# Cross-attention block: scores in 32x64 tiles, value products in 64x32 tiles, maxima spread through DRAM

## The chip, the core and the metric

The kernel runs on one core of a Trainium2 chip. The metric is the time of one execution on the device in microseconds (us). The core has a matrix engine (TensorE, "PE" in the profile, its weight loads "PEld"), a vector engine (VectorE, "DVE"), an activation engine (ScalarE, "ACT"), a general engine (GpSimd, "POOL") and a queue that issues DMAs (SyncE, "SP"). Each engine takes its instructions in the order of the program and waits at the first whose inputs or buffers are not ready. TensorE writes to PSUM only, here eight banks of 128 x 512 floats.

## What is computed

One cross-attention layer in 32-bit floats. `x` is 16 x 1024 x 512, the context 16 x 64 x 512, and there are 16 heads of 32 features.

```python
xq  = ada_ln(x, cond)                 # normalise, then scale and shift by the condition
xkv = ada_ln(context, cond)
q = (xq @ Wq + bq)                    # (16, 1024, 16 heads, 32)
k, v = split(xkv @ Wkv + bkv)         # (16, 64, 16 heads, 32) each
scores = einsum('bqhd,bkhd->bhqk', q, k) / sqrt(32)
attn = softmax(scores)
out = einsum('bhqk,bkhd->bqhd', attn, v)
return x + (out @ Wp + bp)
```

## The kernel before

The queries are worked on in 32 blocks of 512 rows, two to a batch element. A block `i` passes through these steps:

- `load_x`, `q_stats`, `q_scale`, `hidden`: load the rows, take mean and variance (DVE), make the reciprocal deviation (a few tiny steps on ACT and POOL), normalise (ACT, L335).
- `turn`, `move`: transpose 32x32 pieces on DVE (L365) and put them together with 16 DMAs of 64 KB (L387), so that features lie on partitions. `scale_features` (ACT, L447) applies the condition.
- `query_product(i, 1..7)` (L539): q = xq Wq by seven half-size products instead of eight (Strassen's scheme), 4 matmuls of 128x128x256 each. POOL makes the sums that this needs (`feature_sums`, L498). `query_seed`, `query_out` (ACT) and `query_added` (DVE, L585) collect the parts.
- `scores(i, z)`: the 64 keys are taken in two halves z of 32. `score_products` (L658) runs 16 matmuls of a 32x32 tile for each half: row group r and column group c of the array hold one head each, so the 128 output partitions are 4 heads x 32 keys. `maximum` (DVE, L675) reduces over the 32 keys of each head while it transposes 32x32 pieces, and `copied` (ACT, L684) moves the scores to SBUF.
- `maxima`: the larger of the two halves (`both`, L695), spread again over 32 partitions by a transpose of a repeated operand into one 128x2048 tile (L704). `subtract` (POOL, L717) takes it from both halves, `weights` (ACT, L723) makes the exponentials.
- `total` (POOL, L757) adds the two halves, `row_total` (DVE, L762) sums over keys, `inverse_rows` takes the reciprocal and sends it through DRAM to the partitions of the output, `spread_rows` (L788) spreads it.
- `mix` (L826): 32 matmuls in 32x32 tiles, the two halves of the keys added in PSUM. `divided` (DVE, L806) scales them out of PSUM.
- `row_sums` (POOL, L930 to L935), `product(i, 1..7)` (L955), `added` (DVE, L979): the projection, again seven products, added to the residual and stored.

PSUM has two double banks "s", which scores and value products take in turn, and four single banks: 0 and 1 for the query products, 2 and 3 for the projection. The order of all work is written out by hand and the engines take it as it stands. The loop over `i` from 3 to 29 issues, for TensorE and with a = i-1, b = i-2, n = i+1, f = i+2 (numbers are the seven products):

```text
scores(i,0)  product(b,6)  query(n,1)  scores(i,1)  product(b,5)  product(b,4)
query(n,2)   product(b,3)  mix(a)      query(n,6)   product(a,1)  product(a,2)
query(n,7)   query(n,5)    query(n,4)  query(n,3)   product(a,7)
```

Blocks 0 to 2, the context keys and values and the last two blocks stand ahead of and behind the loop; block 29 is projected by four full products (`project`).

The two code paths that the change touches most read, before:

```python
for c in range(NC):
    nc.tensor.matmul(pss[r // 2][32 * c : 32 * c + 32, r % 2, :],
                     lhsT=kt[rows, c, z * HK : (z + 1) * HK], rhs=qt[rows, c, :], ...)
both(m, m_tiles.pop(i), ALU.max)
mb_tiles[i] = spread(i, m, f"mb_{i}", other=i == NB - 1)
```

Of the kernel before, what the change touches and what calls it, by code (L numbers as in the profile page):

```python
# [15 lines left out]
P = 128  # L16
# [4 lines left out]
def cross_attention_block(  # L21
# [566 lines left out]
    V_all = {g: kvpool.tile([P, PER, 2, P], F32, tag=f"V{g}", name=f"V_{g}") for g in GROUPS}  # L588
    for g, at in GROUPS.items():
        for bl in range(PER):  # L590
            k_tiles[at * PER + bl] = K_all[g][:, :, bl * LKV : (bl + 1) * LKV]
            v_tiles[at * PER + bl] = V_all[g][:, bl]
# [16 lines left out]
    def value_places(i, m, h, k):  # L609
        if i not in stages:  # L610
            stages[i] = wpool.tile([P, NT, H], F32, tag="WT", name=f"stage_{i}")
        dst = stages[i][:, 2 * h : 2 * h + 2, m * HO : (m + 1) * HO]
        return qa["v", k].rearrange("p (t f) -> p t f", t=2), dst

    def value_out(i, n):
        k, m, h = OUTS[n]
        src, dst = value_places(i, m, h, k)
        b = b_v_sb[:, m * HO : (m + 1) * HO]
        nc.vector.tensor_tensor(dst, src, b.unsqueeze(1).to_broadcast([P, 2, HO]), ALU.add)
# [6 lines left out]
    def value_move(i, m):  # L626
        for c in (2 * m, 2 * m + 1):
            for j in range(2):
                for z in range(2):
                    at = j * LKV + z * HK  # L630
                    nc.sync.dma_start(  # L631
                        V_all[i][32 * c : 32 * c + 32, j::2, z, :],
                        stages[i][at : at + HK, :, c * P : (c + 1) * P],
                    )
# [16 lines left out]
    def score_products(i, z):  # L651
# [3 lines left out]
        for r in range(HPC):  # L655
            rows = slice(32 * r, 32 * r + 32)
            for c in range(NC):
                nc.tensor.matmul(  # L658
                    pss[r // 2][32 * c : 32 * c + 32, r % 2, :],
                    lhsT=kt[rows, c, z * HK : (z + 1) * HK],  # L660
                    rhs=qt[rows, c, :],
                    start=True,
                    stop=True,
                )
        if z == 0:
            m_tiles[i] = small.tile([P, 2, HPC, NJ], F32, tag="m2", name=f"m2_{i}")
# [7 lines left out]
    def maximum(i, z, e):  # L674
        nc.vector.tensor_reduce(  # L675
            m_tiles[i][:, z, 2 * e : 2 * e + 2, :],
# [16 lines left out]
    def both(dst, src, op):  # L693

        nc.vector.tensor_reduce(dst, src.rearrange("p z r j -> p (r j) z"), AX.X, op)  # L695

    def spread(i, src, name, other=False):
        if other:

            t = qpool.tile([P, 4, NC, NT * 32], F32, tag="xt", name=name)  # L700
            t = t.rearrange("p g c n -> p (g c n)")
        else:
            t = rpool.tile([P, HPC * TB], F32, tag="spread", name=name)
        nc.vector.transpose(t, src.unsqueeze(2).to_broadcast([P, HPC * NJ, 32]))  # L704
        return t.rearrange("p (r q) -> p r q", r=HPC)

    mb_tiles = {}

    def maxima(i):

        m = small.tile([P, HPC * NJ], F32, tag="m", name=f"m_{i}")
        both(m, m_tiles.pop(i), ALU.max)
        mb_tiles[i] = spread(i, m, f"mb_{i}", other=i == NB - 1)

    def subtract(i, eng=nc.gpsimd, zs=(0, 1)):
        for z in zs:
            eng.tensor_tensor(s_tiles[i, z], s_tiles[i, z], mb_tiles[i], ALU.subtract)  # L717
# [3 lines left out]
    def weights(i, z):  # L721
        p = s_tiles[i, z]
        nc.scalar.activation(p, p, AF.Exp, scale=SCALE)  # L723

    def sums(i, z):
        if z == 0:
            l_tiles[i] = small.tile([P, 2, HPC, NJ], F32, tag="l2", name=f"l2_{i}", bufs=1)
        nc.vector.tensor_reduce(
            l_tiles[i][:, z],
            s_tiles[i, z].rearrange("p r (j a) -> p r j a", a=32),  # L730
# [5 lines left out]
    vb_tiles = {}  # L736

    def inverse(i):

        v = small.tile([P, HPC * NJ], F32, tag="v", name=f"v_{i}")  # L740
        both(v, l_tiles.pop(i), ALU.add)
        nc.vector.reciprocal(v, v)
        vb_tiles[i] = spread(i, v, f"vb_{i}", other=i == NB - 1)

    def divide(i, eng=nc.gpsimd):
        vb = vb_tiles.pop(i)
        for z in range(2):
            eng.tensor_tensor(s_tiles[i, z], s_tiles[i, z], vb, ALU.mult)


    sum_tiles, lt_tiles, vt_rows = {}, {}, {}

    def total(i):

        pool, tag = (xpool, "x") if i == NB - 2 else (big, f"big{(i + 1) % 2 * 2}")
        t = pool.tile([P, HPC, TB], F32, tag=tag, name=f"sum_{i}")
        nc.gpsimd.tensor_tensor(t, s_tiles[i, 0], s_tiles[i, 1], ALU.add)  # L757
        sum_tiles[i] = t

    def row_total(i):  # L760
        lt_tiles[i] = small.tile([P, HPC, NJ], F32, tag="lt", name=f"lt_{i}")
        nc.vector.tensor_reduce(  # L762
            lt_tiles[i],
            sum_tiles.pop(i).rearrange("p r (j a) -> p r j a", a=32),
            AX.X,
            ALU.add,
            apply_transpose=True,
        )

    def halves_total(i):  # L770
        lt_tiles[i] = small.tile([P, HPC, NJ], F32, tag="lt", name=f"lt_{i}")
        both(lt_tiles[i].rearrange("p r j -> p (r j)"), l_tiles.pop(i), ALU.add)

    def inverse_rows(i):

        lt = lt_tiles.pop(i)
        nc.vector.reciprocal(lt, lt)
        v = small.tile([P, NC, NJ], F32, tag="vr", name=f"vr_{i}")
        d = dram.tile([NC, 32, HPC, NJ], F32, tag="lt", name=f"ltd_{i}")
        nc.sync.dma_start(d.rearrange("c a r j -> (c a) r j"), lt)  # L780
        for r in range(HPC):
            nc.sync.dma_start(v[32 * r : 32 * r + 32], d[:, :, r, :].rearrange("c a j -> a c j"))
        vt_rows[i] = v

    def spread_rows(i):
        v = vt_rows.pop(i).rearrange("p c j -> p (c j)")
# [6 lines left out]
    def divided(i):  # L793
        vb = vb_tiles.pop(i)
        pool, tag = (big, "big2") if i == NB - 2 else (opool, "ot")
        ot = pool.tile([P, NC, TB], F32, tag=tag, name=f"ot_{i}")
        ot_tiles[i] = ot
        po = po_tiles.pop(i)
        for e in range(len(po)):
            if len(po) == NC:  # L800
                nc.vector.tensor_tensor(ot[:, e, :], po[e], vb[:, e, :], ALU.mult)
                if e < 2:
                    biased(i + 1, 2 + e)
            else:
                cs = slice(2 * e, 2 * e + 2)
                nc.vector.tensor_tensor(ot[:, cs, :], po[e], vb[:, cs, :], ALU.mult)  # L806
# [3 lines left out]
    def mix(i, apart=True, ks=(None,) * NC):  # L810
# [10 lines left out]
        for z in range(2):  # L821
            p = s_tiles.pop((i, z))
            for c in range(NC):
                rows = slice(32 * c, 32 * c + 32)
                for r in range(HPC):
                    nc.tensor.matmul(  # L826
                        po[c][32 * r : 32 * r + 32, :],
                        lhsT=vt[rows, z, 32 * r : 32 * r + 32],
# [784 lines left out]
```

## Time and profile before

| | |
|---|---|
| median of 2 runs | 1030.69 us (1029.12 to 1032.26) |
| the profiled execution | 1030.86 us, of which the span from first to last instruction is 1029.1 |
| PE busy | 1009.3 us, 8077 matmul passes |
| DVE, ACT, POOL busy | 860.9, 638.6, 805.9 us |
| DMA | 149.82 MB, mean 146 GB/s |
| granted clock of TensorE | 0.998 |

Busy time is the union of an engine's instructions. A 32-bit matmul appears as two records, one for each pass. Behind a group stand its count, its busy time, the mean of one instruction in ns and the idle time of the engine just before it, with what ended that.

### The profile page before, as it was taken

The numbers are of one execution on the slowest core, as the hardware profiler recorded it, in microseconds if no ns is written. First come the engines' busy times: TensorE is split into PE (matmuls) and PEld (weight loads), VectorE is DVE, ScalarE is ACT, GpSimd is POOL, SyncE is SP. The second block draws the span as 40 slices with busy tenths as digits, with TensorE's granted clock in tenths as the row PEclk, the third lists the DMA queues.
The fourth block names the chain that finished last, engine by engine and source line by source line (L and its number), as shares of the span: only waits on it lengthen the run. The fifth ranks groups of instructions, "written<-read, shape, count | busy, mean of one in ns | idle before, by whom it ended". The sixth has DMA issues, their size and how long they took to land.

```text
span 1029.1 us, 21212 instructions
## 1 busy us (share of the span) xinstructions
PE 1009.3 (98%) x8077; PEld 763.4 (74%) x8077; DVE 860.9 (84%) x1174; ACT 638.6 (62%) x1025; POOL 805.9 (78%) x518
## 2 busy tenths in 40 slices
PE   8999899999999999999999999999999999999998
PEld 7877556777777777777777778777777777777746
DVE  6686669889888888889898888898888888876795
ACT  3786565666666666667666666666666676665530
POOL 4566687798888888898888888988888888987861
PEclk9999999999999999999999999999999999999999
DMA  9563544444544444445444444445434444335122
GB/s 318 179 188 119 149 122 136 157 157 156 165 155 121 143 128 154 152 152 166 140 134 146 150 133 153 156 159 165 148 110 151 134 154 154 113 125 166 46 85 85
DMA packets 112197, 149.82 MB, mean 146 GB/s; under 512 B 34104, under 2 KB 45392, under 8 KB 112096
## 3 DMA queue, kind: packets, MB, share of 16 engines
q1 hardware_dynamic: 111712, 147.94, 45.3%
q8 instruction: 64, 1.05, 0.4%
q0 software_dynamic: 384, 0.54, 0.3%
q14 instruction: 37, 0.30, 0.1%
HBM read 79.21 MB, written 34.60 MB: 111 GB/s over the span
## 4 chain that ended last, share of the span: by engine, by line
PE 81%; SPq 6%; DMA 5%; DVE 4%; ACT 1%; issue 1%; POOL 1%; DVEq 0%; ACTq 0%; POOLq 0%
PE pp L955 34%; PE pq L539 33%; PE po L826 6%; PE ps L658 6%; SPq L387 4%; DMA ltd<-lt 1%; SPq L631 1%; PE pk_A L539 1%; PE pv_A L539 1%; DMA xt<-ht 1%; DMA r<-in_x_dram 1%; DVE ht L365 1%; DVE lt L762 1%; DMA wss_kv<-in_L_xcond_Wss_kv_dram 1%; DMA x<-in_x_dram 1%
## 5 line engine op out<-in xcount | busy, mean ns | idle before, releaser
L717 POOL TENSOR_TENSOR s<-s,mb 128x2048 f32<-128x2048 f32 x64 | 290.2, 4558 | 129.3 <-DVE mb L704 127.7
L684 ACT COPY s<-ps 128x1024 f32<-128x1024 f32 x128 | 129.4, 1012 | 108.1 <-DVE m L675 64.8
L675 DVE TRANSPOSE_TENSOR_REDUCE m<-ps 128x32 f32<-128x1024 f32 x128 | 150.7, 1213 | 33.6 <-PE ps L658 33.4
L955 PE MATMUL pp<-w_p_sb,ot 128*128 128x256 f32 x720 | 165.6, 379 | 0.5 <-DVE r L979 0.4
L979 DVE TENSOR_TENSOR r<-pp,r 128x512 f32<-128x512 f32 x203 | 131.8, 670 | 30.9 <-PE pp L955 24.3
L578 ACT ACTIVATE qt<-pq,bias_t 128x256 f32<-128x256 f32 x256 | 105.6, 463 | 77.2 <-PE pq L539 77.0
L955 PEld LDWEIGHTS pp<-w_p_sb,ot 128*128 128x128 f32 x720 | 136.6, 190 | 20.5 <-issue 1.6
L723 ACT ACTIVATE s<-s 128x2048 f32<-128x2048 f32 x64 | 122.3, 1911 | 43.8 <-POOL s L717 43.8
L757 POOL TENSOR_TENSOR sum<-s,s 128x2048 f32<-128x2048 f32 x31 | 140.7, 4540 | 7.0 <-ACT s L723 7.0
L955 PEld LDWEIGHTS pp<-WT,s 128*128 128x128 f32 x480 | 86.5, 189 | 57.0 <-issue 37.7
L539 PE MATMUL pq<-xt_sums,w_q_sums 128*128 128x256 f32 x512 | 123.3, 385 | 0.0
L539 PE MATMUL pq<-xt,w_q_sums 128*128 128x256 f32 x512 | 121.1, 379 | 1.6 <-DVE qt L585 1.6
L539 PE MATMUL pq<-xt,w_q_sb 128*128 128x256 f32 x512 | 121.6, 380 | 0.3 <-ACT pq L551 0.2
L539 PEld LDWEIGHTS pq<-xt_sums,w_q_sums 128*128 128x128 f32 x512 | 94.9, 190 | 36.5 <-issue 24.8
L955 PE MATMUL pp<-WT,s 128*128 128x256 f32 x480 | 119.3, 391 | 0.2 <-POOL s L934 0.2
L955 PE MATMUL pp<-WT,ot 128*128 128x256 f32 x480 | 113.6, 379 | 0.6 <-POOL ot L931 0.6
L539 PEld LDWEIGHTS pq<-xt,w_q_sb 128*128 128x128 f32 x512 | 96.8, 190 | 16.4 <-issue 1.7
L539 PEld LDWEIGHTS pq<-xt,w_q_sums 128*128 128x128 f32 x512 | 97.2, 190 | 15.2 <-DVE qt L585 2.0
L955 PEld LDWEIGHTS pp<-WT,ot 128*128 128x128 f32 x480 | 91.0, 190 | 14.1 <-POOL ot L931 1.0
L335 ACT ACTIVATE x<-x,rstdq 128x512 f32<-128x512 f32 x128 | 97.0, 807 | 4.4 <-POOL rstdq L312 4.4
L447 ACT ACTIVATE xt<-xt,ss_q 128x512 f32<-128x512 f32 x124 | 93.9, 808 | 5.1 <-DMA xt<-ht 4.5
L498 POOL TENSOR_TENSOR xt_sums<-xt 128x512 f32<-128x512 f32 x64 | 81.4, 1272 | 14.2 <-ACT xt L447 7.3
(176 smaller groups left out, 1509.8 us busy)
## 6 DMA issues: line engine op xcount, KB each, us to landing
x<-in_x_dram SPq DMA_DIRECT2D x32, 1024.0 KB, 5.5
r<-in_x_dram SPq DMA_DIRECT2D x32, 1024.0 KB, 5.1
xt<-ht SPq DMA_DIRECT2D x488, 64.0 KB, 2.0
out_dram<-r SPq DMA_DIRECT2D x58, 512.0 KB, 3.7
out_dram<-r SPq DMA_DIRECT2D x11, 256.0 KB, 2.2
wss_kv<-in_L_xcond_Wss_kv_dram SPq DMA_DIRECT2D x4, 512.0 KB, 7.3
wss_q<-in_L_xcond_Wss_q_dram SPq DMA_DIRECT2D x4, 512.0 KB, 11.0
vr<-ltd SPq DMA_DIRECT2D x128, 8.0 KB, 1.6
```

What stands on the lines that cost most here:

```text
L335: nc.scalar.activation(dst, src, AF.Identity, bias=rstd[:, 1, j : j + 1], scale=rstd[:, 0, j : j + 1])
L447: nc.scalar.activation(xt[:, :, c, :], xt[:, :, c, :], AF.Identity, scale=ss["q"][:, c, b : b + 1], bias=ss["q"][:, NC + c, b : b + 1],)
L498: eng.tensor_tensor(dst, a, b, ALU.subtract)
L539: nc.tensor.matmul(out_, lhsT=lhsT, rhs=rhs, start=new and m == 0 and c == 0, stop=c == HC - 1, skip_group_check=True,)
L578: nc.scalar.activation(dst, src, AF.Identity, bias=bq_t[:, o : o + 1])
L675: nc.vector.tensor_reduce(m_tiles[i][:, z, 2 * e : 2 * e + 2, :], s_banks[i, z][e].rearrange("p r (j a) -> p r j a", a=32), AX.X, ALU.max, ...
L684: nc.scalar.copy(s_tiles[i, z][:, 2 * e : 2 * e + 2, :], s_banks[i, z][e])
L717: eng.tensor_tensor(s_tiles[i, z], s_tiles[i, z], mb_tiles[i], ALU.subtract)
L723: nc.scalar.activation(p, p, AF.Exp, scale=SCALE)
L757: nc.gpsimd.tensor_tensor(t, s_tiles[i, 0], s_tiles[i, 1], ALU.add)
L955: nc.tensor.matmul(acc[k][:, t * HO : (t + 1) * HO], lhsT=rows[:, c, t * P : (t + 1) * P], rhs=cols[:, c, :], start=n == 2 and t == 0 and ...
L979: nc.vector.tensor_add(r, a, r)
```

## The change

Scores and value products use larger tiles, and the heads are divided in another way.

- A score half is now two groups of heads over all 64 keys, not all heads over 32 keys. Half `z` takes chunks z and 2+z of the features: 8 matmuls of 32 rows x 64 columns. The value product has 64 rows (keys) x 32 columns: 16 matmuls in place of 32, with nothing added up in PSUM. The value tiles are laid out to match, in 4 larger DMAs a group instead of 16.
- A head's 64 keys lie on two 32-partition groups. `maxima(i, w)`, now called for each half, copies the neighbouring group's maxima over (two copies of 32x64), takes the larger, transposes 128x64 (L709), stores it in DRAM by two DMAs (L712), and `spread_maxima` reads it back by two DMAs (L719) that repeat a row for 64 partitions, into the single tile "spread". The transpose of 128x2048 is gone; only for the last block (`wide`) the old way is kept, with four copies.
- `total` is gone. `sums` (DVE, L736) runs on each half; `rows_out`, `rows_in` carry the sums through DRAM, and `inverse` (L762, L766) adds the two groups and takes the reciprocal afterwards.
- The output of `mix` is no longer scaled on its way out of PSUM by DVE. `mixed` copies it (ACT, L818), two instructions a block, and `scaled` multiplies (POOL, L822).
- `product(b, 2)` starts from a copy of bank 2 (`product_seed`, ACT, L896).
- The projection of a block runs a whole loop step after its value product: `mix(a)` stands in the middle of the step, all seven products of `b` around it. Block 29 takes the seven products like the others. The order of blocks 0 to 2, the context and the end is written anew.

```diff
     def score_products(i, z):
-            for c in range(NC):
+            for u in range(2):
                 nc.tensor.matmul(
-                    pss[r // 2][32 * c : 32 * c + 32, r % 2, :],
-                    lhsT=kt[rows, c, z * HK : (z + 1) * HK],
-                    rhs=qt[rows, c, :],
+                    pss[r // 2][LKV * u : LKV * (u + 1), r % 2, :],
+                    lhsT=kt[rows, 2 * u + z, :],
+                    rhs=qt[rows, 2 * u + z, :],
...
+    pair = const.tile([P, HPC * NJ], F32, name="pair")
+    def maxima(i, w, wide=False):
+        m2 = m_tiles.pop((i, w)).rearrange("p r j -> p (r j)")
+        m = small.tile([P, HPC * NJ], F32, tag="m", name=f"m_{i}_{w}")
+        for k in range(4):
+            if wide or k % 2 == 0:
+                o = k + 1 - 2 * (k % 2)
+                nc.vector.tensor_copy(pair[32 * k : 32 * k + 32], m2[32 * o : 32 * o + 32])
+        nc.vector.tensor_tensor(m, m2, pair, ALU.max)
+        if wide:
+            t = rpool.tile([P, HPC * TB], F32, tag="spread", name=f"mb_{i}_{w}")
+            nc.vector.transpose(t, m.unsqueeze(2).to_broadcast([P, HPC * NJ, 32]))
+            mb_tiles[i, w] = t.rearrange("p (r q) -> p r q", r=HPC)
+            return
+        mt = small.tile([P, 2, 32], F32, tag="mt", name=f"mt_{i}_{w}", bufs=2)
+        nc.vector.transpose(mt.rearrange("p h a -> p (h a)"), m)
+        d = dram.tile([2, 2, 32, 32], F32, tag="m", name=f"md_{i}_{w}")
+        for u in range(2):
+            nc.sync.dma_start(d[u].rearrange("h x a -> x h a"), mt[LKV * u : LKV * u + HK])
+    def spread_maxima(i, w):
+        d = m_rows.pop((i, w)).rearrange("u h x a -> u (h x a)")
+        t = rpool.tile([P, HPC * TB], F32, tag="spread", name=f"mb_{i}_{w}")
+        for u in range(2):
+            nc.sync.dma_start(
+                t[LKV * u : LKV * (u + 1)], d[u : u + 1].to_broadcast([LKV, HPC * TB])
+            )
...
     def mix(...):
-        for z in range(2):
-            for c in range(NC):
-                rows = slice(32 * c, 32 * c + 32)
+        for w in range(2):
+            for u in range(2):
+                rows = slice(LKV * u, LKV * (u + 1))
                 for r in range(HPC):
                     nc.tensor.matmul(
-                        po[c][32 * r : 32 * r + 32, :],
-                        lhsT=vt[rows, z, 32 * r : 32 * r + 32],
+                        po[2 * u + w][32 * r : 32 * r + 32, :],
+                        lhsT=vt[rows, w, 32 * r : 32 * r + 32],
                         rhs=p[rows, r, :],
-                        start=(z == 0),
-                        stop=(z == 1),
+                        start=True,
+                        stop=True,
                     )
+    def mixed(i, e):
+        nc.scalar.copy(ot_tiles[i][:, 2 * e : 2 * e + 2, :], po_tiles[i][e])
+    def scaled(i, e):
+        ot, vb = (t[i][:, 2 * e : 2 * e + 2, :] for t in (ot_tiles, vb_tiles))
+        nc.gpsimd.tensor_tensor(ot, ot, vb, ALU.mult)
```

The new loop step, engine by engine:

```text
PE    query(n,1) scores(i,0) query(n,2) product(b,1) scores(i,1) query(n,6) query(n,7)
      product(b,2) query(n,5) product(b,6) product(b,7) mix(a) query(n,3)
      product(b,5) product(b,4) product(b,3) query(n,4)
DVE   maximum(i,0,1) statistic maximum(i,0,0) maxima(i,0) sums(a,1) maximum(i,1,0)
      maximum(i,1,1) maxima(i,1) statistic added(b,2) 2 statistics 3 turns added(b,6)
      query_added(n,5) added(b,7) turn inverse(a) added(b,5) spread_rows(a) sums(i,0)
      added(b,4) query_added(n,4) added(b,3)
ACT   query_seed(n) biased(b,2) copied(i,0,0) copied(i,0,1) weights(a,1) product_seed(b)
      query_out(n,2) copied(i,1,1) hidden query_out(n,6) copied(i,1,0) hidden scale
      query_out(n,7) 2 scales biased(b,3) hidden scale weights(i,0) q_scale query_out(n,3)
      mixed(a,0) mixed(a,1) hidden
POOL  row_sums(b,0) row_sums(b,1) subtract(i,0) 3 feature_sums(f) q_scale subtract(i,1)
      scaled(a,0) feature_sums(f) scaled(a,1)
SP    md(i,0) x2, mb(i,0) x2, ltd(a), md(i,1) x2, residual(a), vr(a) x4, mb(i,1) x2,
      x(i+5), move(i+3) x16, out(b) x2
```

Each `row_sums` is two instructions; the second of `row_sums(b,1)` overwrites what product(b,2) reads and waits for it. `scores(i+1,0)` needs `query_added(i+1,4)`.

## The prediction

> **What bounds the kernel now.** I read the page first: the busy shares, then the chain that ended last.
>
> ```profile
> PE 1009.3 (98%) x8077; PEld 763.4 (74%) x8077; DVE 860.9 (84%) x1174; ACT 638.6 (62%) x1025; POOL 805.9 (78%) x518
> ...
> PE 81%; SPq 6%; DMA 5%; DVE 4%; ACT 1%; issue 1%; POOL 1%; DVEq 0%; ACTq 0%; POOLq 0%
> ```
>
> TensorE hardly idles and most of the chain is its own. A window of one block of the loop says the same. Behind the stretch stand its length and the busy time of PE, PEld, DVE, ACT and POOL:
>
> ```profile
> 544.04:573.22 29.18, 29.18 (x241) 22.30 (x240) 25.87 (x35) 19.16 (x31) 24.38 (x16) 1.00 0.48 153
> ```
>
> The score matmuls of blocks 4 and 30 start at 193.74 and 952.75, so a block takes 759.0 / 26 = 29.19 us. What fills it, from TensorE's timeline (start, length, count):
>
> ```profile
> 571.42 1.89 PE L955 MATMUL pp<-WT,ot 128*128 128x256 f32 x8
> 573.24 1.14 PE L658 MATMUL ps<-qt,K_B 32*32 32x512 f32 x32
> 574.31 0.48 PE L955 MATMUL pp<-WT,s 128*128 128x256 f32 x1
> ...
> 584.32 1.89 PE L955 MATMUL pp<-WT,ot 128*128 128x256 f32 x8
> 586.14 2.35 PE L826 MATMUL po<-s,V_B 32*32 32x512 f32 x64
> ```
>
> One wide product (8 records: 4 matmuls of two passes) follows another every 1.727 us, so 14 of them take 24.18. A score half takes 1.07 (573.24 to 574.31), and the wide products before and after it are 0.09 and 0.11 longer: 1.27. The product with the values takes 2.28 and the same 0.2: 2.47. 24.18 + 2 x 1.27 + 2.47 = 29.19: TensorE is the bound. GpSimd waits 127.7 / 31 = 4.1 us per block:
>
> ```profile
> POOL s L717 <- DVE mb L704: 127.7, 31, 8.6
> ```
>
> **The change, part by part.** S is the start of a block's scores.
>
> *Tiles.* In a score half the 16 first passes start 6.7 ns apart, the second passes 0.454 after them, the next product 0.516 after the last: 0.454 + 0.100 + 0.516 = 1.07. Eight tiles, still 512 columns in two passes, shorten the middle term to 0.05: a half costs 1.22. The value product has two such rounds; the old second round began 0.52 after the last pass of the first. Eight tiles save between 0.13 (two shorter skews, other gaps kept) and 0.43 (that gap closed); I take 0.27, so 2.20. No 32x64 tile is in the trace: were the two tiles of a row group to run one after the other, a half would cost two more passes, 0.85. By TensorE alone: 24.18 + 2.44 + 2.20 = 28.82 us per block, 0.37 less.
>
> *Work moved.* Per block DVE loses the spreading transpose (2.24), the two halves' maximum (0.30) and the two scalings out of PSUM (2.28), and gains one sum (2.24) and two `maxima` of four small instructions, 0.16 to 0.20 each by L237 and L316, 0.8 each: 25.9 becomes about 24.9. ACT gains two 0.91 copies and a 0.5 seed: 21.5. POOL trades one 4.54 addition for two scalings of half the size: even. DMA gains 2 MB, 72 GB/s over 29 us beside 153, and SP 8 issues of about 0.43, which its queue (16 moves at 0.63) has room for. All lies under TensorE.
>
> *The wait it adds.* `subtract` now waits for maxima that go to DRAM and back. From the end of `maxima`: a store like `ltd<-lt` (1.5 us), then two 512 KB reads, which I put at 5.0 together (1 MB loads land in 5.1): 6.7 with the issues. The upper bank's maximum ends at S + 4.6 (1.34 after the scores, 1.13, a 0.9 statistic, 1.21). Without hindrance `maxima` ends at S + 5.4 and the first subtraction could start at S + 12.1; POOL is only free at S + 12.6, after the last row sum, which waits for product 2. Behind it in POOL's queue stand three feature sums, the second subtraction, both scalings and the next row sums, with 4 us of slack. So far it is hidden.
>
> *What takes the cover away.* While the context keys are made, DVE and POOL both run two-input operations on SBUF, POOL's first and DVE's second:
>
> ```profile
> 22.90 1.72 POOL L472 TENSOR_TENSOR w_k_sums<-w_k_sums,w_k_sb 128x512 f32<-128x512 f32 x1
> 24.57 1.72 POOL L472 TENSOR_TENSOR wv_sums<-wv_sums,w_v_sb 128x512 f32<-128x512 f32 x1
> ...
> 27.93 1.27 POOL L472 TENSOR_TENSOR w_k_sums<-w_k_sb,w_k_sums 128x512 f32<-128x512 f32 x1
> ```
>
> ```profile
> 24.01 1.16 DVE L498 TENSOR_TENSOR xk_sums_A<-xk_A 128x512 f32<-128x512 f32 x1
> 25.20 1.64 DVE L498 TENSOR_TENSOR xk_sums_A<-xk_A,xk_sums_A 128x512 f32<-128x512 f32 x1
> ```
>
> DVE's operations end at 25.17 and 26.84, both times 0.55 after POOL's instruction in progress ended (24.62, 26.29): they stood still until then. POOL's take 1.72 in place of 1.27: they waited for DVE. The two take turns. In today's loop no DVE instruction reads two SBUF operands. In the new `maxima` the maximum (L702) does and will be blocked. For its two 32x64 copies (L701) there is no row: at the low end 0.17 (L237, also one SBUF input), at the high end one POOL instruction each, 1.3 beside the row sums. The nearest large row is this one-input SBUF operation:
>
> ```profile
> 11.51 0.54 DVE L344 TENSOR_SCALAR x_A<-x_A,rstdq 128x512 f32<-128x512 f32 x1
> ```
>
> It takes 0.54 for 512 elements where a statistic (L294) takes 0.68: (0.54 - 0.17) / 504 is 0.73 ns an element, faster than the 1.0 of one an element in the other rows, so it reads SBUF more broadly than they do. I take the high end.
>
> The Trainium skill ("SBUF — State Buffer", Who interferes with whom) says that copies of this kind can also enter a mode that takes the ports shared with GpSimd for the whole instruction; the trace shows this for two inputs (the 0.55 above), not for a copy. By that rule the sum is 1100; were only two-input operations blocked, 1030.
>
> *The walk.* POOL ends the last scaling near S + 3.9, then runs three row sums of 1.3. The first copy is issued at S + 4.6 and goes at 5.2, the second at 6.65, the maximum at 8.1; `maxima` ends at 8.45, not 5.4. Two loops follow.
> - DVE to ACT to PE: sums to 10.7, next maximum to 11.85, then on ACT a copy 0.91, normalise 0.71, scale 0.71, query output 0.71, two scales 1.41, `biased` 0.52: 16.9. TensorE is at product 7 at S + 14.55: a stall of 2.35, a block of 31.2.
> - POOL: the subtraction starts at 8.45 + 6.7 = 15.15; then 4.5, 4.0 (feature sums), 1.1, 4.5, 2.3, 1.3, 2.3 = 20.0 to the last scaling; then 4.55 to the end of the next `maxima` and 6.7: 31.25.
> I take 31.2: 2.0 more than now.
>
> *The ends.* Scores of block 3 start at 162.6 now, those of block 31 at 974.3, and 54.8 remain. The new start lacks three products of block 1 and has one query product more (-3.5), the tiles save 0.8, blocked maxima cost some 2.7: 161. The end: the value product comes later and no query work is left to cover, so TensorE stands about 8 us before product 7 of block 29 (the last maxima wait for the first subtraction), 3.5 before product 1 of block 30 and 2 to 3 elsewhere. By the order of the list and the durations above that is 63, with blocking 64. 161 + 28 x 31.2 + 64 = 1098.6. The profiled run is 1030.86 for a span of 1029.1 (median of the runs 1030.69), so 1.8 lies around it: **1100**.
>
> **The rivals.**
> - *Only the maximum is blocked.* `maxima` ends near 5.8, POOL keeps slack, blocks take 28.82: 158.3 + 807 + 63 + 1.8 = 1030. For it: small copies are short (L237); the GpSimd slack of 4.1. Against: L344. 0.25; 1018 to 1045.
> - *Faster.* Small tiles lose the 0.2 around a half and the value product comes to 1.75: 28.0 a block, shorter end: 158 + 784 + 59 = 1001. It decides if `maxima` ends before S + 6 as well. Against it the skew terms. 0.05.
> - *A collision with the subtraction.* The second `maxima` starts at S + 12.95, 2.2 before the 4.5 us subtraction. Were the spread to land 2.2 earlier, a copy would wait 4.5 and the maximum another 1.35: product 7 at 21.9, blocks of 36: 161 + 1008 + 66 = 1235. 0.08.
> - *The tiles do not overlap.* 0.85 on each of four rounds: 32.2 a block, 158 + 902 + 63 = 1123. 0.05; every small tile in the trace overlaps.
>
> **How the numbers follow.** The forecast has 0.57. Its own range is 1062 (both copies pass in one turn: 30.0 a block, 1065) to 1150 (reads 1.8 slower). The range leaves out the faster case, the collision and a little of the first rival, 0.16: 1022 to 1160. A measurement here tells about 2% from no change (1010 to 1051): faster 0.06, same 0.24, slower 0.70.
>
> **What would show it.** L701 and L702 with means of 0.6 to 1.5 us while POOL is busy, 0.2 while it idles; TensorE idle before L931 (product 7), released by ACT's `pp` copy; a period near 31; POOL waiting for DMA `mb`. Copies of 0.2 throughout and a period under 29 would prove me wrong, as would value products above 2.5.

## The result and the profile after

The kernel after takes 1207.24 us (median of 2 runs, 1206.82 to 1207.66) against 1030.69: 1.171 times as long, 95% interval 1.163 to 1.179. It is slower, as forecast, but by 177 us and not by 69; 1100 was recorded, with 1160 as the upper end.

The page of the kernel after, first the busy shares and then the chain that ended last:

```profile
PE 1063.8 (88%) x6053; PEld 781.2 (65%) x6053; DVE 953.2 (79%) x1345; ACT 703.8 (58%) x1117; POOL 798.4 (66%) x545
...
PE 36%; DVE 22%; DMA 21%; POOL 13%; issue 3%; ACT 3%; SPq 3%; POOLq 0%; DVEq 0%; ACTq 0%
```

TensorE's share of the chain fell from 81% to 36%; DVE, DMA and POOL hold 56%. No single engine is busy all the time: this is the look of a ring, in which each waits for another once per block. The window over 26 blocks of the loop (start of the scores of block 4 to those of block 30; columns: length, then busy time of PE, PEld, DVE, ACT and POOL, granted clock, DMA share, GB/s):

```profile
231.94:1099.59 867.65, 785.88 (x4577) 582.12 (x4577) 735.04 (x995) 549.52 (x843) 635.01 (x409) 0.96 0.71 191
```

A block takes 867.65 / 26 = 33.37 us, where it took 29.19. PE is busy for 785.88 / 26 = 30.23 of it and idle for 3.14. TensorE's own work was to be 28.82 by the forecast; the last experiment below runs blocks in 28.73. So the 4.18 us are: -0.46 for the tiles, +1.50 for slower products, +3.14 for idling.

Three stretches tell where the 176.7 us between the two spans went. Here and in the table of runs, "start" is the time at which the scores of block 3 begin, "block" is the time from there to the scores of block 31 divided by 28, and "end" is the rest of the span:

| | start | block | end |
|---|---|---|---|
| before | 162.6 | 28.99 | 54.8 |
| forecast for the change | 161 | 31.2 | 64 |
| after | 196.6 | 33.26 | 77.9 |

The forecast missed 35.6 in the start, 57.7 in the loop and 13.9 at the end.

The small instructions of `maxima` stood still, as forecast. First the groups of the two lines (behind the bar: busy time, mean of one in ns; then idle time before them), then a block on DVE and on POOL (start, length):

```profile
L701 DVE COPY pair<-m 32x64 f32<-32x64 f32 x132 | 95.1, 720 | 3.1
L702 DVE TENSOR_TENSOR m<-m,pair 128x64 f32<-128x64 f32 x64 | 71.9, 1124 | 2.2
```

```profile
703.04 2.83 DVE L701 COPY pair<-m 32x64 f32<-32x64 f32 x2
705.91 2.30 DVE L702 TENSOR_TENSOR m<-m,pair 128x64 f32<-128x64 f32 x1
708.24 0.25 DVE L709 STREAM_TRANSPOSE mt<-m 128x64 f32<-128x64 f32 x1
```

```profile
702.25 2.35 POOL L822 TENSOR_TENSOR ot<-ot,vb 128x1024 f32<-128x1024 f32 x1
704.56 1.27 POOL L498 TENSOR_TENSOR xt_sums<-xt,xt_sums 128x512 f32<-128x512 f32 x1
705.78 2.35 POOL L822 TENSOR_TENSOR ot<-ot,vb 128x1024 f32<-128x1024 f32 x1
708.09 1.26 POOL L908 TENSOR_TENSOR s<-ot 128x512 f32<-128x512 f32 x1
```

The first copy ends with the first scaling (704.6), the second with the feature sum (705.8), the maximum with the second scaling (708.1). One POOL instruction each, in turns. But the instructions met are the scalings of 2.35, not the row sums of 1.3: the last scaling ends 9.2 us after S in the mean of blocks 4 to 29, where I had S + 3.9. Over the same blocks the first `maxima`, from the first copy to the end of the maximum, take 4.63 us in the mean, the second 0.91, and 0.65 where POOL is idle.

What TensorE waits for is not what I forecast. From the list of waits (total, times, longest):

```profile
PE pp L931 <- POOL ot L822: 76.5, 27, 5.4
PE pp L931 <- ACT pp L890: 20.9, 12, 8.8
```

The wait for ACT's `pp` copy ahead of product 7 is there, but small; the large one is product 1, which waits for the first scaling on POOL. That stands behind the second subtraction, and both subtractions wait for `mb` from DRAM (`POOL s L725 <- DMA mb<-md` 117.0 us, before 127.7 for DVE's spread). From the end of the transpose at 708.49 to the subtraction at 718.31 the trip takes 9.8 us, where I had 6.7:

```profile
718.31 4.57 POOL L725 TENSOR_TENSOR s<-s,mb 128x2048 f32<-128x2048 f32 x1 [2.24 <-DMA mb<-md]
```

### The profile page after: what moved, and what is told of

The parts are those of the page before. It is cut to its first block, busy times and chain, and to the rows that moved or that the text cites. A ratio compares the mean times of both kernels' runs of the same rounds, so it can differ in the third digit from the quotient of the medians.

```text
span 1205.8 us, 17690 instructions
## 1 busy us (share of the span) xinstructions
PE 1063.8 (88%) x6053; PEld 781.2 (65%) x6053; DVE 953.2 (79%) x1345; ACT 703.8 (58%) x1117; POOL 798.4 (66%) x545
## 3 DMA queue, kind: packets, MB, share of 16 engines
HBM read 145.27 MB, written 36.67 MB: 151 GB/s over the span
## 4 chain that ended last, share of the span: by engine, by line
PE 36%; DVE 22%; DMA 21%; POOL 13%; issue 3%; ACT 3%; SPq 3%; POOLq 0%; DVEq 0%; ACTq 0%
PE pp L931 15%; PE pq L539 12%; POOL s L725 10%; DMA mb<-md 7%; DVE m L671 6%; DVE pair L701 4%; DMA md<-mt 4%; DMA ltd<-l 4%; DMA x<-in_x_dram 4%; PE ps L655 3%; DVE m L702 3%; DVE l L736 3%; POOL ot L822 3%; PE po L803 2%; PE pv_A L539 1%
## 5 line engine op out<-in xcount | busy, mean ns | idle before, releaser
L725 POOL TENSOR_TENSOR s<-s,mb 128x2048 f32<-128x2048 f32 x64 | 290.3, 4537 | 232.6 <-DMA mb<-md 117.0
L931 PE MATMUL pp<-w_p_sb,ot 128*128 128x256 f32 x744 | 203.8, 423 | 82.6 <-POOL ot L822 76.5
L931 PEld LDWEIGHTS pp<-w_p_sb,ot 128*128 128x128 f32 x744 | 153.2, 210 | 119.4 <-POOL ot L822 87.8
L671 DVE TRANSPOSE_TENSOR_REDUCE m<-ps 128x32 f32<-128x1024 f32 x128 | 153.8, 1223 | 42.5 <-PE ps L655 35.6
L955 DVE TENSOR_TENSOR r<-pp,r 128x512 f32<-128x512 f32 x180 | 120.3, 670 | 58.2 <-PE pp L931 57.9
L736 DVE TRANSPOSE_TENSOR_REDUCE l<-s 128x64 f32<-128x2048 f32 x64 | 145.4, 2272 | 10.5 <-ACT s L731 10.5
L822 POOL TENSOR_TENSOR ot<-ot,vb 128x1024 f32<-128x1024 f32 x58 | 136.2, 2349 | 7.2 <-DVE vb L772 7.2
L931 PE MATMUL pp<-WT,ot 128*128 128x256 f32 x496 | 120.8, 387 | 17.3 <-ACT pp L890 17.3
L539 PE MATMUL pq<-xt,w_q_sb 128*128 128x256 f32 x512 | 127.9, 394 | 0.9 <-ACT qt L578 0.9
L447 ACT ACTIVATE xt<-xt,ss_q 128x512 f32<-128x512 f32 x124 | 98.5, 825 | 17.7 <-DMA md<-mt 8.2
L335 ACT ACTIVATE x<-x,rstdq 128x512 f32<-128x512 f32 x128 | 105.1, 828 | 2.9 <-POOL rstdq L312 2.9
L931 PEld LDWEIGHTS pp<-WT,s 128*128 128x128 f32 x496 | 94.6, 191 | 15.2 <-DVE v L766 1.7
```

What stands on the lines that cost most here:

```text
L335: nc.scalar.activation(dst, src, AF.Identity, bias=rstd[:, 1, j : j + 1], scale=rstd[:, 0, j : j + 1])
L447: nc.scalar.activation(xt[:, :, c, :], xt[:, :, c, :], AF.Identity, scale=ss["q"][:, c, b : b + 1], bias=ss["q"][:, NC + c, b : b + 1],)
L539: nc.tensor.matmul(out_, lhsT=lhsT, rhs=rhs, start=new and m == 0 and c == 0, stop=c == HC - 1, skip_group_check=True,)
L671: nc.vector.tensor_reduce(m_tiles[i, z][:, 2 * e : 2 * e + 2, :], s_banks[i, z][e].rearrange("p r (j a) -> p r j a", a=32), AX.X, ALU.max, ...
L725: eng.tensor_tensor(s_tiles[i, w], s_tiles[i, w], mb_tiles.pop((i, w)), ALU.subtract)
L736: nc.vector.tensor_reduce(l_tiles[i][:, :, w, :], s_tiles[i, w].rearrange("p r (j a) -> p r j a", a=32), AX.X, ALU.add, apply_transpose=True,)
```

## The experiments

Each run in one table; "time" is the median of the runs made, a single run where no interval is named here or below (`rows_before`: 1.192 times the time of before, 1.187 to 1.198). Start, block and end are of the profiled execution alone; they add up to its span, which is about 1.8 us under that execution's own time (1123.82 for `moves_in_four_one_input`).

| run | time | start | block | end |
|---|---|---|---|---|
| after | 1207.24 | 196.6 | 33.26 | 77.9 |
| one_input | 1201.56 | 195.7 | 33.27 | 72.4 |
| one_input_copies | 1205.3 | 197.6 | 33.36 | 71.6 |
| one_input_max | 1208.54 | 198.3 | 33.44 | 72.0 |
| rows_before | 1235.01 | 198.9 | 34.26 | 76.5 |
| x_last | 1302.76 | 197.4 | 36.73 | 75.2 |
| x_last_one_input | 1298.11 | 197.4 | 36.70 | 71.3 |
| act_queue | 1302.62 | 201.1 | 36.67 | 73.0 |
| act_queue_one_input | 1221.1 | 201.2 | 33.77 | 72.4 |
| x_act_wide_ends | 1262.61 | 194.0 | 35.50 | 72.5 |
| x_act_one_input_wide_ends | 1236.97 | 182.4 | 35.10 | 69.6 |
| four_moves_more | 1272.78 | 201.1 | 35.61 | 72.7 |
| moves_in_four | 1176.75 | 193.7 | 32.33 | 77.6 |
| moves_in_four_one_input | 1128.15 | 193.1 | 30.64 | 71.0 |
| moves_in_four_rows_before | 1229.68 | 195.5 | 34.16 | 76.0 |
| moves_in_four_rows_before_one_input_wide_ends | 1078.67 | 181.3 | 29.49 | 69.8 |
| before_four_moves_more | 1053.74 | 164.9 | 29.72 | 54.8 |
| before_moves_in_four | 1021.89 | 155.7 | 28.91 | 55.0 |
| before_start_two_queues | 1032.00 | 163.1 | 29.02 | 54.8 |

### Are the blocked instructions the loss?

My first theory was the recorded one, enlarged by the trip. The edit replaces what can be blocked by reductions over one SBUF input:

```diff
...
-                nc.vector.tensor_copy(pair[32 * k : 32 * k + 32], m2[32 * o : 32 * o + 32])
-        nc.vector.tensor_tensor(m, m2, pair, ALU.max)
+                nc.vector.tensor_reduce(pair[32 * k : 32 * k + 32],
+                    m2[32 * o : 32 * o + 32].unsqueeze(2), AX.X, ALU.max)
+        nc.vector.tensor_reduce(m, pairs_[:, w].rearrange("p z m -> p m z"), AX.X, ALU.max)
```

> Edit: the copies and the maximum of `maxima` become reductions with one SBUF input, the same number of instructions. Theory A (two causes in one ring: the blocked first maxima of a block, 4.5 us instead of 0.65, and two trips of the maxima through DRAM, 9.8 and 7.4 us, all ahead of the scaling that product 1 of the next block waits for): first maxima 0.7 to 0.9 us, ring 4 shorter, period about 30.5 instead of 33.5, time about 1120 (1095 to 1145). Rival B (the DRAM trips alone make the ring, DVE only waits beside them): maxima as short, but time above 1185. Rival C (what I recorded: blocked maxima are all of the loss in the loop): period 28.8, time below 1085.

> Edit: only the two 32x64 copies become one-input reductions, the maximum stays a two-input operation. Theory A: the reductions take 0.2 us, the maximum waits for one GpSimd instruction (1 to 2.3 us); first maxima about 2.5 us, time about 1160. If only the maximum were blocked and the copies just came behind it, this would be as slow as 1195 to 1207.

> Edit: only the maximum becomes a one-input reduction, the two copies stay copies. Theory A: the first copy waits for GpSimd's instruction in progress, the second for one more; first maxima about 2.9 us, time about 1165. If copies do not take the shared ports, first maxima are 0.8 us and the time is that of the kernel with all three replaced.

The instructions behave as expected: the three reductions take 0.207, 0.214 and 0.290 us in the median and 0.294 at most, the first `maxima` 0.76 in place of 4.63. With the copies alone replaced they take 1.70, with the maximum alone replaced 3.09 (blocks 4 to 29). So the copies do contend, and 3.9 us of waiting per block are gone. And the time is almost the same: 1.162 times that of before (1.159 to 1.166), the block 33.27 as it was, and most of the 6 us come from the end. Theory A falls as far as the loop goes, and the recorded explanation with it; the result is where rival B had it (above 1185). The single runs of the two halves lie within 2 us of the kernel after, where some 1160 was expected.

The transpose of the maxima on DVE and SP's queue in `one_input` show why (start, length, number):

```profile
670.50 0.24 DVE L710 STREAM_TRANSPOSE mt<-m 128x64 f32<-128x64 f32 x1
...
673.88 1.07 SPq L958 DMA_DIRECT2D out_dram<-r  x2
675.04 2.05 SPq L713 DMA_DIRECT2D md<-mt  x2
```

The maxima are transposed at 670.74, but SP issues their store at 675.04: until then it is busy with the 16 moves and the output of the block before. In the kernel after the store is issued at 708.52, 0.03 after the transpose ends, but in both kernels the two stores have landed a median of 0.36 us after the 512 KB output that was issued just ahead of them. In the median of blocks 4 to 29 the store is issued 9.7 us after S in the kernel after and 9.5 in `one_input`: blocked or not, the maxima did not leave earlier.

### The queue as the ring

One turn of SP's queue in the kernel after, from one read of the second maxima to the next:

```profile
722.91 1.09 SPq L719 DMA_DIRECT2D mb<-md  x2
724.10 0.53 SPq L119 DMA_DIRECT2D x<-in_x_dram  x1
724.73 13.80 SPq L387 DMA_DIRECT2D xt<-ht  x16
738.62 1.43 SPq L957 DMA_DIRECT2D out_dram<-r  x2
741.04 1.25 SPq L712 DMA_DIRECT2D md<-mt  x2
743.66 1.12 SPq L719 DMA_DIRECT2D mb<-md  x2
...
755.34 1.09 SPq L719 DMA_DIRECT2D mb<-md  x2
```

The read at 722.91 waits until the subtraction (718.31 to 722.88) has freed the only `spread` tile. Then: from that read's issue to the moves 1.82, 16 moves 13.89, output 2.42 (the last 1.0 is a wait for the blocked maxima), store of the next maxima 2.62, their read 6.94 (it lands at 750.60), the next subtraction 4.74: 32.43 in all. Sixteen issues of 0.63 make 10.1, not 13.9. SP's own waits name the rest:

```profile
SPq L387 <- DMA x<-in_x_dram: 76.7, 28, 4.4
SPq L387 <- DMA mb<-md: 40.4, 26, 1.9
```

The seventh move starts when the second read of `mb` has landed, the eighth when x has: each was issued eight places before it. In blocks 4 to 29 of the kernel after, none of 849 issues starts before the one eight places earlier has landed, and 51 start within 0.06 us of that; 111 start before the one seven places earlier has. The limit is the program's: the trace shows its issues using eight semaphores in turn, each waiting on its semaphore until the transfer that used it before has landed. Two runs tried to unload the queue by another order or another queue, with and without the blocked instructions:

> Edit: in the loop `load_x(i + 5)` is issued behind the 16 moves instead of ahead of them. Theory D (formed from the runs so far: the ring is SP's queue, in which the store of the next block's maxima stands behind the load of x and 16 moves; an issue begins only when the transfer eight issues before it has landed, so the 8th move waits for the 1 MB of x): the moves end about 4 us earlier, the store then waits for the maxima instead, period 30 to 32, time 1110 to 1165. Theory E (the 16 DMA engines, 0.71 to 0.75 busy, are the bound): the order of issues changes nothing, time above 1190.

> Edit: as the run before, and the copies and the maximum of `maxima` as one-input reductions. Theory D: with the moves out of the way, the blocked maxima are next in the ring, so what gave 5 us alone gives 20 to 45 us here, time 1080 to 1130. Theory E: time above 1185. If the blocked maxima never matter: the same time as the run before within 10 us.

> Edit: the stores and the reads of the maxima are issued from ACT's queue instead of SP's. Theory D: SP's ring is open; the ring that is left goes through the blocked maxima, the two trips and GpSimd (32 by its terms), time 1120 to 1180; SP no longer waits for GpSimd. ACT loses some 4 us per block in issues and waits. Theory E: above 1190.

> Edit: as the run before, and one-input reductions in `maxima`. Theory D: period about 30, time 1080 to 1130, 30 us or more under the run before. Theory E: above 1185.

Both edits brought a new wait and were slower. With x behind the moves the statistics of DVE, which stand between the two maxima of a block, wait for it:

```profile
DVE bs L294 <- DMA x<-in_x_dram: 158.8, 26, 10.4
```

With the maxima's transfers on ACT's queue, ACT stands still at them (105.7 us of idle time ahead of its exponentials alone), and there the blocked copies cost 82 us: 36.67 a block with them, 33.77 without. All four lie above what theory D expected of them, in the range of E, but each has a new wait that may put it there: these runs don't tell theories D and E apart. `rows_before`, made with the first three, has the same fault:

> Edit: in the loop each block subtracts the maxima of the block before it (the stores and the reads are the same in number and size; the softmax keeps its value, but the maxima subtracted are not the block's own). So no subtraction waits for this block's maxima, only for the read after the single buffer is free. The copies and the maximum stay as they are. Theory A: period 29 to 31, time 1080 to 1140. Rival C (blocked maxima are the loss, by DVE and ACT to product 7): period above 32.5, time above 1175. Rival B: period 28.8 to 29.2, time below 1085.

It missed theory A's range too (34.26 a block). Its reads of the first maxima stand behind the 16 moves on SP, so it moved the queue too; it is taken up below. A third way to open the queue failed more instructively:

```diff
...
-        if i + 5 < NB: load_x(i + 5)
+        if i + 5 < NB: load_x(i + 5, nc.scalar)
```

> Two edits in different stretches, read apart by the starts of the scores. (1) In the loop x is loaded from ACT's queue, so the moves no longer wait for its landing. Theory D: period 31.0 to 32.7 instead of 33.3, where the blocked maxima are next. Theory E: 33 or more. (2) Blocks 0 to 2 and 28 to 30 spread their maxima by the transpose on DVE, without the trip through DRAM (DVE gets 2.2 us for each). If the trip is what made the start and the end long: scores of block 3 start at 165 to 180 instead of 196.6, and what remains from the scores of block 31 is 60 to 70 instead of 78. If it is not, both stay within 6.

> The same two edits and one-input reductions in `maxima`. Theory D: period 29.5 to 30.8, at least 1.2 under the run before. If the blocked maxima never matter in the loop: the same period within 0.3.

Theory D missed both blocks, 35.50 and 35.10. With the spread on DVE alone the start falls by 2.6 us and the end by 5.4, so the trip by itself did not make them long. The moves waited for x all the same, and longer: the eight semaphores serve both queues, and x is now issued later.

```profile
SPq L387 <- DMA x<-in_x_dram: 167.4, 27, 7.8
```

With the waits for `mb` (40.4 us before, 12.0 here) the moves stand still for 62 us more in all, and 28 blocks are 63 us longer. That speaks for D, but only the next runs test it.

### A dose, and a shorter queue

```diff
+        for g in range(4) if i >= 6 else ():
+            nc.sync.dma_start(xt[0:32, g], ht[32 * g : 32 * g + 32, 0].rearrange("p c t b -> p c (t b)"))
```

> Edit: in the loop 4 of the 16 moves `xt<-ht` are issued a second time behind the others (same data, same place), 25 times. Theory D (SP's queue is the ring): each costs its issue, 0.6 us, so 2.4 us a block and 60 us in all (45 to 75). Theory E (the 16 DMA engines are the bound): 0.25 MB on some 6.8 MB a block, at 200 GB/s 1.3 us a block, 15 to 35 us. If neither is the ring: within 12 us.

> Edit: the same four repeated moves in the kernel before. Theory D: SP had room there, the time stays within 10 us of the kernel before.

The dose costs 65.5 us, 2.35 a block, against 60 and 2.4 expected from the issue time alone. In the kernel before it costs 0.73 a block, 20.6 us over 28 blocks (17.7 against the kernel before as measured beside it, 1036.05): more than the 10 that I allowed, and ACT waits 41.7 us there for the later moves (4.5 without the dose), but less than a third of what it costs after. Then the opposite:

```diff
-            for g in range(4):
-                (nc.gpsimd if two and g % 2 else nc.sync).dma_start(
-                    xt[32 * k : 32 * k + 32, g],
-                    ht[32 * g : 32 * g + 32, k].rearrange("p c t b -> p c (t b)"))
+            (nc.gpsimd if two and k % 2 else nc.sync).dma_start(
+                xt[32 * k : 32 * k + 32].rearrange("p g c n -> p (g c n)"),
+                ht[32 * k : 32 * k + 32].rearrange("p g c t b -> p (g c t b)"))
```

> Edit: the 16 moves `xt<-ht` of 64 KB become 4 of 256 KB: the same bytes in a quarter of the issues. They put the pieces of the queries' features at other places than the kernel needs, so the values are not the reference's; shapes, engines and all waits are kept. Theory D (SP's queue is the ring: 16 issues of 0.63, one of which stands still until the 1 MB of x eight issues before it has landed): SP gets about 9 us a block, the ring that is left goes through the blocked maxima, two trips and GpSimd: period 31 to 32.5, time 1135 to 1185. Theory E (the bytes are the bound): above 1195.

> As the run before (values not the reference's for the same reason), and one-input reductions in `maxima`. Theory D: now the blocked maxima are on the ring, and taking them away, which gave 5 us in the kernel after, gives 30 to 70: period 29.5 to 30.7, time 1085 to 1140. If the blocked maxima never matter: within 10 us of the run before.

> The same four larger moves in the kernel before (values not the reference's for the same reason). Theory D: SP is not its ring, within 12 us of the kernel before.

All three came out inside what Theory D expected: 1.139 times the time of before (1.136 to 1.142), 1.092 (1.088 to 1.096) and 0.989 (0.987 to 0.991). The block falls to 32.33, and with one-input reductions to 30.64: what gave 6 us alone gives 49 now. The same bytes move, and faster (196 and 208 GB/s in the loop in place of 191, at a busy share of the DMA engines of 0.74 and 0.79 in place of 0.71), so the DMA engines were not the bound. Whether the time of an issue or the wait for a semaphore weighed more is not told apart: four moves have less of both. In `moves_in_four` both waits of TensorE that I had recorded or seen are there:

```profile
PE pp L930 <- POOL ot L821: 54.1, 27, 5.5
PE pp L930 <- ACT pp L889: 34.3, 22, 9.1
```

and without the blocked instructions the second is gone from the loop (the two that are left stand at the end, 7.8 and 3.6 us), while product 1 still waits for the scaling behind the trip (`moves_in_four_one_input`):

```profile
PE pp L931 <- POOL ot L822: 41.5, 23, 3.2
PE pp L931 <- ACT pp L890: 11.4, 2, 7.8
```

### Without the trip

The last pair takes the trip off the ring, once with the blocked instructions and once without:

```diff
...
-        d = m_rows.pop((i, w)).rearrange("u h x a -> u (h x a)")
+        d = m_rows[i - (4 <= i < NB - 4), w].rearrange("u h x a -> u (h x a)")
...
```

The reads are also issued earlier: those of the second half a little earlier in the step, those of the first half at the end of the step before, behind the moves.

> Edit: the four larger moves (values not the reference's) and, in the loop, the maxima of the block before subtracted, so that no subtraction waits for this block's trip through DRAM; copies and maximum as in the kernel after. Against the run with the four moves alone (period 32.3): Theory D says that the waits of product 1 for the scaling go, and what is left is the recorded loop by DVE and ACT to product 7 (1.65 us of waiting in the trace of the four moves, 2.35 recorded): period 30 to 31.2, time 1095 to 1145. If the trip is not on the ring: period above 31.8.

> As the run before (values not the reference's), with one-input reductions, and blocks 0 to 2 and 28 to 30 spread by DVE without DRAM. Theory D: trip, SP's queue and blocked instructions are all off the ring, TensorE's own 28.7 is the bound: period 28.7 to 29.5. Scores of block 3 start at 178 to 183 instead of 193; the rest of the way to the 155.7 of the kernel before with the same moves is the new order of the start. Tail 66 to 71. Time 1050 to 1085. A period above 30 means a cause that I have not named.

The first expectation was wrong, by 85 us and in sign: 34.16 a block, slower than with the trip. By its own words that would take the trip off the ring, but the trace shows another wait. The timeline on DVE, POOL and PE:

```profile
615.67 5.14 DVE L700 COPY pair<-m 32x64 f32<-32x64 f32 x2
```

```profile
615.01 1.27 POOL L912 TENSOR_TENSOR ot<-ot,s 128x512 f32<-128x512 f32 x1 [2.96 <-PE pp L930]
616.24 4.51 POOL L724 TENSOR_TENSOR s<-s,mb 128x2048 f32<-128x2048 f32 x1
```

```profile
623.45 3.78 PE L930 MATMUL pp<-WT,ot 128*128 128x256 f32 x8 [5.13 <-ACT pp L889]
```

With nothing to wait for, the subtraction starts at 616.24, as the second `maxima` begin; the second copy takes 4.47 us, nearly the whole of the subtraction's 4.51, and product 7 waits 5.1. From block 3 to 30, the 17 blocks in which a copy or the maximum takes over 3 us are 35.7 to 37.1 us long; the other eleven are 29.6 to 33.1, six of them 29.8. This is the recorded rival "a collision with the subtraction", at its price ("blocks of 36"); copies of up to 4.47 us stand in the trace of `rows_before` (34.26) as well. In `moves_in_four` the second `maxima` had ended at 663.8 and the subtraction began at 667.13: the trip had kept them apart.

Without the blocked instructions the block is 29.49, and the most common length is 28.73 (scores of blocks 7, 8 and 9 at 300.13, 328.86 and 357.59). From block 4 to 30:

```profile
211.50:975.88 764.38, 751.86 (x4578) 571.69 (x4577) 639.41 (x1003) 548.71 (x843) 639.69 (x410) 1.00 0.81 211
```

TensorE is busy for 751.86 of 764.38 at full clock: the bound is its own work again, and with queue, trip and blocked instructions taken away together all but 0.7 us a block of what the change lost in the loop is gone. The start comes to 181.3, the end to 69.8.

The kernel before had gained 7 us at its start with four larger moves. A version that issues half of the moves of blocks 2 and 3 from GpSimd was to keep a part of that with the right values:

> Edit in the kernel before: every second of the moves of blocks 2 and 3, in the start, is issued from GpSimd's queue, as those of block 1 are already. With four larger moves this kernel started the scores of block 3 at 155.7 instead of 162.6. If that gain came from SP's issues at the start, half of it is had here with the right values: scores of block 3 at 157 to 161, time 2 to 6 us under the kernel before. Against it stand eight issues of about 0.5 us on GpSimd for each block: if GpSimd is late there, no change or up to 4 us more.

It gave nothing (0.9995, 0.9985 to 1.0005; start 163.1). So issues on SP alone are not what the 7 us were. No version with the right values beat the kernel before.

## Why the prediction was right in sign and wrong in size

- **Blocked copies and maximum: right as a mechanism, wrong in its place.** Copies of 32x64 took 0.18 to 3.6 us, those that were blocked one POOL instruction each, with the maximum in turn. That settles the recorded rival in which only the maximum is blocked. The Trainium skill ("SBUF — State Buffer", Who interferes with whom) has copies among the operations that can contend with GpSimd and two-input operations among those that do, and on trn2 reductions never; the runs agree (0.206 to 0.294 for the reductions of `one_input` in every block). But in the kernel after, the loss from it in the loop is nil (33.26 and 33.27). It is 1.7 a block once SP's queue is short (32.33 and 30.64), and 4.7 once the trip is gone too (34.16 and 29.49; the second of these runs also spreads the last blocks on DVE).
- **The step that failed is "SP 8 issues of about 0.43, which its queue (16 moves at 0.63) has room for".** I added up issue times; I didn't walk SP's queue as I walked POOL's and DVE's. The second read waits there for the first subtraction, and the load of x, 16 moves and the output stand behind it and ahead of the next store of maxima. The waits for the transfer eight issues earlier add 3.8 in the turn shown (13.9 less 16 x 0.63). With the queue short, the block falls by 0.93: 26 of the 57.7 us that the forecast missed in the loop.
- **The trip was mis-sized.** "6.7 with the issues" measured 9.8 in the block shown: 2.4 for a store of 8 KB, and 7.4 for the two reads that I put at 5.0. The median of a read is 6.3, and of the whole trip of the first half 10.7 (blocks 4 to 29). The second read, from the buffer's release to its landing, took 7.2, so it is not hidden behind 5 us of feature sums.
- **The period of 31.2 was near 32.33 for the wrong reasons.** In `moves_in_four` one turn of POOL took 31.33 (635.80 to 667.13, the first subtractions of two blocks); recorded was 31.25. But from the subtraction to the end of the last scaling it is 22.5, not 20.0, because of the second read; and from there to the next subtraction 8.9, not 11.25, since the blocked `maxima` end together with that scaling and not 4.55 after it. Two errors of 2.4 cancelled. TensorE is busy for 29.71 a block in that run, 0.98 over its own 28.73, at a granted clock of 0.98; how much of the 1.1 between 31.2 and 32.33 this makes was not tested.
- **No term for the clock.** A wait was priced at its length. The products after it are slow as well: 1.50 us a block. From block 4 to 30 of the kernel after the trace has the clock at one half for 64.8 us, in 17 stretches; half of that is 1.25 us a block. In the same part of the kernel before it is never below full.
- **The tiles: right.** The score half lasts 1.05 from its first matmul to the next product (698.58 to 699.63), with the same 0.19 around it 1.24; recorded 1.22. The product with the values is 1.88 and 0.19, 2.07; recorded 2.20. TensorE's own block is 28.73; recorded 28.82, before 29.19. Neither "the tiles do not overlap" nor "faster" had a case.

```profile
698.58 1.11 PE L655 MATMUL ps<-qt,K_B 32*64 32x512 f32 x16
699.63 1.99 PE L539 MATMUL pq<-xt,w_q_sb 128*128 128x256 f32 x8
...
719.76 1.95 PE L803 MATMUL po<-s,V_B 64*32 64x512 f32 x32
721.64 1.99 PE L539 MATMUL pq<-xt,w_q_sums 128*128 128x256 f32 x8
```

- **The start (196.6 for 161) was hardly worked out**: I counted products and added 2.7 for the blocked maxima. Trip and blocked instructions together cost 14.2 there (182.4 without both; 195.7 with one-input reductions alone, 194.0 with the spread on DVE alone). Four larger moves beside that give 181.3. The other 21 were not taken apart, and their cause stays open. The order there is new, the store of the row sums lands in 6.1 us (median, 64 KB; 1.5 for the 32 KB before), and TensorE is busy for 158.0 of 181.3 us.
- **The end (77.9 for 64)**: the two large waits are there as recorded, 8.8 ahead of product 7 (8 recorded) and 3.6 ahead of product 1 (3.5). Not recorded are 5.4 ahead of block 29's product 1, which is the loop's wait, and the slow clock: PE is busy for 53.2 of 77.9 us at a clock of 0.84, 50.1 at 0.90 in the last experiment, for the same matmuls.

## What to carry to other kernels

A queue that issues DMAs is an engine: when a change puts a transfer on the path from one step to the next, walk that queue for a whole period with every wait in it, the transfers still under way included. Removing a wait that the trace shows plainly may give nothing as long as another ring has the same length; take the suspects away together and in both orders before naming a price. And a wait can protect: without the trip through DRAM the subtraction ran into the copies, and the kernel became slower.

## What the hardware showed that I had not expected

- At most eight transfers of SP and ACT were under way in this program: 0 of 849 issues in blocks 4 to 29 started before the one eight places earlier had landed, and a load from ACT's queue counted with SP's. The eight semaphores that the issues take in turn set this; whether the queues would take more is not shown.
- A small store did not overtake a large one: the two stores of 8 KB had landed 0.36 us (median) after the 512 KB issued ahead of them; the first took 3.08 us from its issue in the loop of the kernel after and 1.36 in `moves_in_four`, where the output had been issued 9 us earlier.
- Waits of TensorE cost more than their length. In the loop of the kernel after, 28 products of the projection waited for more than 1 us. The 6 that followed waits of up to 1.94 us ran their eight passes in 1.92 us, measured to the start of what follows; of the 22 after longer waits, 17 took 2.3 to 3.7. The mean clock granted over each of these 17 was 0.50 to 0.80, over each of the others 1.00. Two such products:

```profile
704.65 2.58 PE L931 MATMUL pp<-w_p_sb,ot 128*128 128x256 f32 x8 [3.03 <-POOL ot L822]
```

```profile
671.82 3.19 PE L932 MATMUL pp<-w_p_sb,ot 128*128 128x256 f32 x8 [3.62 <-POOL ot L823]
```

The first is from the kernel after, the second from `one_input`; undisturbed products have a printed length of 1.89.
